# A four-layer network on one core: the last half batch leaves in two parts of 256 positions

## The chip, the cores and the metric

The kernel runs on one core of one Trainium2 chip. The core has five engines with a queue of instructions each: TensorE (PE, matrix products), VectorE (DVE), ScalarE (ACT), GpSimd (POOL) and SyncE (SP, which here issues the transfers). They wait for one another through semaphores. The metric is the time of one execution on the device in microseconds (us), lower is better. A trace of one profiled execution gives the start and the duration of each instruction; its span runs from the first to the last instruction.

## The reference, cut to what matters

The input is x of 8 batches, 512 channels and 32 x 32 = 1024 positions, fp32. Four layers follow one another. Layer 0 is an attention over 64 channels with a batch norm over the whole input, layer 1 a full attention over the positions, layers 2 and 3 are:

```python
# layer 2: t, p, g = the three projections of x (128 channels each)
s = softmax(t.T @ p * SCALE)
att = s @ g                      # 128 channels x 1024 positions
x = x + (Z_w @ att) * inv + shift
# layer 3
a = sign(x + rsign_bias)
y = (sign(W) * scale) @ a        # 512 x 512
s = batchnorm(y) + x
t = s - pr_shift
out = where(t > 0, t, pr_slope * t) + pr_bias
```

The change lies in the last product of layer 2 (by Z_w) and all of layer 3, for half of the positions of the batch that is worked on last.

## The kernel before, in words

The 512 channels lie as 4 blocks of 128 on the partitions; a position is a column. The 1024 positions are worked on in two halves of 512 columns (`HF`)[...]. `fast` does one batch. The batches come in a fixed order. In all but the last, the end of a batch is mixed with the products of the next batch, so that TensorE always has work. In the last batch (the `else` branch of `fast`, L994 to L1012) there is nothing to mix in but the end itself.

That end is, for each half h:

- `values2` (L954): the sum over positions of g times the exponentials, in one PSUM bank; DVE multiplies it by the inverse of the sums into `att` (L967).
- `close2` (L671): for each of the 4 blocks of channels, a product by z into a bank (L675, fp32; each product is two instructions on TensorE), and on DVE the sum with x, in place in `xt` (L677).
- `leave` (L679), a generator that stops at its `yield`s: 4 Signs on ACT (L686) make `sg` (f16). Then for each pair j of 0 and 1: a buffer `both` with members y1 (block j) and y2 (block j+2), and for each member a product of four f16 matmuls (L698) into a bank of its own. On DVE y = product x scale + x (L719). Then the last layer's rectifier, in one of two ways:
  - by way of POOL: DVE makes `up` (L725, both operands in SBUF), ACT makes y (L728, Identity), POOL adds them (L735), SyncE issues the output (L736);
  - by way of ACT and DVE: ACT makes `up` (L741, Relu), then y (L742, Identity), DVE joins them (L749), SyncE issues the output (L753).

The first way is taken where `h == 0 or j == 0` (L723), so only pair j1 of the second half goes the second way. Its last member y2 is cut in two there (L738, L739), each of 256 positions.

In the last batch the first half's `leave` is called `before`, the second half's `after`. The code's order is: verdict count (`count_bad`, a check of the softmax sums, one DVE group and one tiny product L789, read by L791), first half's Signs and its products j0 y1, j0 y2 and j1 y1, then the last two matmuls of `values2` of the second half with a stop in between, `close2` of the second half, the rest of `before`, and `after`. Within an engine the instructions run in an order that a scheduler makes from the program, with waits on semaphores where data or a buffer is shared.

Buffers that matter: 8 PSUM banks (tag `bank`) used in turn; 8 large buffers of tag `e` (exponentials, then `sg` and `both`); 3 buffers of tag `half_a`, in which `up` lies. A `tc.If` on the verdict follows (L1606); its body isn't run with this input.

Of the kernel before, what the change touches and what calls it, by code (L numbers as in the profile page):

```python
# [8 lines left out]
F32 = mybir.dt.float32  # L9
F16 = mybir.dt.float16  # L10
I32 = mybir.dt.int32
AF = mybir.ActivationFunctionType
ALU = mybir.AluOpType
# [3 lines left out]
P = 128  # L17
B = 8
C = 512
N = 1024  # L20
CC = C // P
NT = N // P
HF = 512
NH = N // HF
# [61 lines left out]
def kernel(  # L86
# [17 lines left out]
    nc = tc.nc  # L104
    mm = nc.tensor.matmul
# [17 lines left out]
    def bank():  # L123
        return psum["bank"].tile([P, HF], F32, tag="bank", name="bank")
# [17 lines left out]
    def half(i):  # L142
        return bass.ts(i, HF)
# [6 lines left out]
    sbw = {}  # L150
# [74 lines left out]
    def col(name, i):  # L225
        return ct[:, COL[name] + i : COL[name] + i + 1]
# [23 lines left out]
    ps3 = const.tile([P, CC], F32, tag="ps3", name="ps3")  # L250
    pb3 = const.tile([P, CC], F32, tag="pb3", name="pb3")
    rb3 = const.tile([P, CC], F32, tag="rb3", name="rb3")
    sa3 = const.tile([P, CC], F32, tag="sa3", name="sa3")
    cb3 = const.tile([P, CC], F32, tag="cb3", name="cb3")
# [413 lines left out]
            yield  # L668
        made.extend((tt, pt, gt))

    def close2(xt, att, h):  # L671

        for oc in range(CC):
            ps = bank()
            mm(out=ps, lhsT=sbw["z"][:, bass.ts(oc, P)], rhs=att, start=True, stop=True)  # L675
            xs = xt[:, oc, half(h)]
            nc.vector.tensor_tensor(xs, ps, xs, ALU.add)  # L677

    def leave(env, xt, dst, halves=range(NH), signs=None, stop=False):  # L679


        small = env["small"]
        for h in halves:
            sg = env["e"].tile([P, CC, HF], F16, tag="e", name="sg")
            for cc in range(CC):
                nc.scalar.activation(  # L686
                    sg[:, cc, :], xt[:, cc, half(h)], AF.Sign, bias=rb3[:, cc : cc + 1]
                )
            if stop:
                yield  # L690
            for j in range(CC // 2):
                both = env["e"].tile([P, 2, HF], F32, tag="e", name="both")
                y1, y2 = both[:, 0, :], both[:, 1, :]

                def product(lt):
                    ps = bank()
                    for cc in range(CC):
                        mm(  # L698
                            out=ps,
                            lhsT=lt[:, cc, bass.ts(j, P)],  # L700
                            rhs=sg[:, cc, :],
                            start=cc == 0,
                            stop=cc == CC - 1,
                        )
                    return ps

                if signs is None:
                    ps = product(sw3)
                    nc.scalar.activation(y2, ps, AF.Identity, bias=round3, scale=1.0 / PACK)
                    nc.vector.tensor_scalar(y2, y2, ROUND, None, ALU.subtract)  # L710
                    nc.vector.scalar_tensor_tensor(y1, y2, -PACK, ps, ALU.mult, ALU.add)
                    sums = y1, y2
                else:
                    sums = [product(signs[0])]
                    yield
                    sums.append(product(signs[1]))

                for y, ps, oc in ((y1, sums[0], j), (y2, sums[1], j + 2)):
                    nc.vector.scalar_tensor_tensor(  # L719
                        y, ps, sa3[:, oc : oc + 1], xt[:, oc, half(h)], ALU.mult, ALU.add  # L720
                    )
                    up = small.tile([P, HF], F32, tag="half_a", name="up3")
                    if signs is not None and (h == 0 or j == 0):  # L723

                        nc.vector.tensor_scalar(  # L725
                            up, y, nc3[:, oc : oc + 1], ps3[:, oc : oc + 1], ALU.max, ALU.mult
                        )
                        nc.scalar.activation(  # L728
                            y,
                            y,  # L730
                            AF.Identity,
                            bias=qb3[:, oc : oc + 1],
                            scale=col("L3_conv_pr_slope", oc),
                        )
                        nc.gpsimd.tensor_tensor(y, y, up, ALU.add)  # L735
                        nc.sync.dma_start(out=dst[:, oc, half(h)], in_=y)  # L736
                        continue
                    final = signs is not None and y is y2  # L738
                    for q in (slice(0, HF // 2), slice(HF // 2, HF)) if final else [slice(0, HF)]:  # L739
                        yq, uq = y[:, q], up[:, q]  # L740
                        nc.scalar.activation(uq, yq, AF.Relu, bias=cb3[:, oc : oc + 1])  # L741
                        nc.scalar.activation(  # L742
                            yq,
                            yq,
                            AF.Identity,
                            bias=pb3[:, oc : oc + 1],
                            scale=col("L3_conv_pr_slope", oc),
                        )
                        nc.vector.scalar_tensor_tensor(  # L749
                            yq, uq, ps3[:, oc : oc + 1], yq, ALU.mult, ALU.add  # L750
                        )
                        to = slice(h * HF + q.start, h * HF + q.stop)
                        nc.sync.dma_start(out=dst[:, oc, to], in_=yq)  # L753
                yield

    def unpacked(env):

        t = env["big"].tile([P, 2 * CC, N], F16, tag="h", name="signs")
        lo, hi = (t[:, i].rearrange("p (cc c) -> p cc c", c=C // 2) for i in range(2))
        near = env["big"].tile([P, 6, HF], F32, tag="hs", name="near")  # L760
        near = near[:, 0:2, :].rearrange("p i (cc c) -> p (i cc) c", c=C // 2)
        nc.vector.tensor_scalar(near, sw3, 1.0 / PACK, ROUND, ALU.mult, ALU.add)
        nc.vector.tensor_scalar(hi, near, ROUND, None, ALU.subtract)
        nc.vector.scalar_tensor_tensor(lo, hi, -PACK, sw3, ALU.mult, ALU.add)
        return lo, hi
# [28 lines left out]
    def channels(ap):  # L794
        return ap.rearrange("(cc p) n -> p cc n", p=P)
# [89 lines left out]
    def fast(env, n, hb, ua):  # L885
# [3 lines left out]
        xt = resident.pop(b)  # L889
# [47 lines left out]
        signs = None  # L937
        if more:
            steps = make_u(env, hb, got)
        else:  # L940
            signs = unpacked(env)

        def fill(k=1):
            for _ in range(k):
                next(steps, None)
# [26 lines left out]
        dst = channels(out[b])  # L972
        fill()
        values2(0, range(0, 2))
        if more:
            r = inverse_sums(env, esum, B + n)
            values2(0, range(2, NTH))
            att = values2(0, range(NTH, NT))
            values2(1, range(0, NTH))
            close2(xt, att, 0)  # L980
            att = values2(1, range(NTH, NT))
            fill()
            for _ in leave(env, xt, dst, [0]):
                fill()
            close2(xt, att, 1)
            rest3.append(leave(env, xt, dst, [1], stop=True))
            next(rest3[0])
            fill(2)
            for _ in steps:
                pass  # L990
        else:


            r = inverse_rows(env, esum, B + n)  # L994
            att = values2(0, range(2, NT))
            values2(1, range(0, 2))
            close2(xt, att, 0)
            values2(1, range(2, 6))
            before, after = leave(env, xt, dst, [0], signs), leave(env, xt, dst, [1], signs)
            count = count_bad(env)  # L1000
            next(count)
            next(before)
            next(before)
            att = values2(1, range(6, NT))
            next(before)
            close2(xt, att, 1)
            for _ in before:
                pass
            next(after)
            next(count)  # L1010
            for _ in after:
                pass  # L1012

        return hb, got[0] if more else None

# [107 lines left out]
    rest = [j for j in range(NPAIR) if j != order[0] // 2]  # L1123
# [6 lines left out]
    env = {}  # L1130
# [105 lines left out]
    for b in range(B):  # L1236
        xt = load_x(b) if b else first
# [145 lines left out]
    ps = bank()  # L1383
# [5 lines left out]
    ps = bank()  # L1389
# [5 lines left out]
    bias, gamma, beta = (ct[:, c0 + 2 * i : c0 + 2 * i + 2] for i in range(3))  # L1395
# [83 lines left out]
    with ExitStack() as main:  # L1479
# [3 lines left out]
        small = main.enter_context(tc.tile_pool(name="small", bufs=3))  # L1483
# [122 lines left out]
    with tc.If(verdict[0] > 0):  # L1606
        with (
# [5 lines left out]
            env = {"big": big, "e": epool, "small": small}  # L1613
# [4 lines left out]
            for b in range(B):  # L1618
                xt = load_x(b)
# [43 lines left out]
```

## Time and profile before

| | |
|---|---|
| time, median of 3 runs | 1901.04 us (1899.94 to 1901.69) |
| the profiled execution's own time | 1901.0 us |
| its span, first to last instruction | 1899.1 us |
| TensorE busy | 1878.7 us (99%), 6178 instructions |
| DVE busy | 1097.8 us (58%), 1762 instructions |
| ACT busy | 510.3 us (27%), 811 instructions |
| POOL busy | 223.5 us (12%), 176 instructions |
| `att` of the last half done (L967) | 1879.70 us |
| last L677 done | 1884.18 us |
| last L719 done | 1890.43 us |
| last L749 done | 1893.62 us |

The busy times are sums over the whole span. The part that the change touches is the last 20 us of it, and there the shares are other ones: between 1884 and 1888 us TensorE is busy 3.89, DVE 3.61, ACT 2.59 and POOL 1.31 of 4 us; between 1888 and 1892 us TensorE 0.26, DVE 3.07, ACT 2.98 and POOL 2.74 of 4 us. A row of a timeline gives start, duration, engine, line, operation and output<-inputs with their shapes, and in brackets the idle time before it with what ended it. `x2` means two instructions merged in one row, from the start of the first to the end of the second. Lines are those of the kernel before.

### The profile page before, as it was taken

Reading aid. Unit: us, or ns where it says so; the run is one execution under the profiler, and the core shown is the slowest. Engines: PE = TensorE matmul, PEld = TensorE weight load, DVE = VectorE, ACT = ScalarE, POOL = GpSimd, SP = SyncE. Lnnn points to the kernel's source line nnn. Section 1 sums busy time; section 2 is a strip of 40 time slices with the busy share of each in tenths; the row PEclk is TensorE's granted clock in tenths of the full one; section 3 lists DMA queues with packets and bytes.
Section 4 is the critical chain, followed back from the end, with each engine's and each line's share of the span. In section 5 each row is a group of like instructions: output and inputs, shape, how many; then the busy total and the mean of one; then the engine's idle time right before and its main releaser. Section 6 shows DMA issues by size and latency. Waiting matters only on the chain.

```text
span 1899.1 us, 16360 instructions
## 1 busy us (share of the span) xinstructions
PE 1878.7 (99%) x6178; PEld 973.4 (51%) x6178; DVE 1097.8 (58%) x1762; ACT 510.3 (27%) x811; POOL 223.5 (12%) x176
## 2 busy tenths in 40 slices
PE   9999999999999999999999999999999999999997
PEld 3366455544745446444645446544645455544653
DVE  3256576457663677438663675457753775466547
ACT  2142222144212432035202421144202521234013
POOL 0000111200121001200121001200130012101121
PEclk9999999999999999999999999999999999999999
DMA  8420000002000110002000110002000200000001
GB/s 322 159 78 6 1 17 1 1 23 78 17 1 1 45 61 12 1 12 89 17 1 0 49 57 12 0 23 78 12 0 12 89 12 0 1 33 22 12 0 47
DMA packets 25203, 66.52 MB, mean 35 GB/s; under 512 B 3552, under 2 KB 4764, under 8 KB 24476
## 3 DMA queue, kind: packets, MB, share of 16 engines
q1 hardware_dynamic: 24188, 64.96, 9.6%
q8 instruction: 51, 0.84, 0.2%
q10 hardware_dynamic: 864, 0.43, 0.1%
q14 instruction: 36, 0.29, 0.1%
q0 software_dynamic: 64, 0.00, 0.0%
HBM read 46.44 MB, written 18.94 MB: 34 GB/s over the span
## 4 chain that ended last, share of the span: by engine, by line
PE 92%; DVE 6%; issue 1%; ACT 1%; DMA 0%; POOL 0%; ACTq 0%; DVEq 0%
PE bank L388 42%; PE bank L557 20%; PE bank L958 6%; PE bank L806 6%; PE bank L1248 5%; PE bank L658 3%; PE bank L675 2%; PE bank L412 2%; PE wide L1288 1%; DVE both L749 1%; DVE both L719 1%; PE bank L1029 1%; PE wide L1342 1%; PE bank L1030 1%; PE bank L698 1%; DVE xt L677 1%
## 5 line engine op out<-in xcount | busy, mean ns | idle before, releaser
L557 PE MATMUL bank<-e,vt 128*128 128x512 f32 x768 | 334.2, 593 | 0.0
L557 PEld LDWEIGHTS bank<-e,vt 128*128 128x128 f32 x768 | 144.9, 190 | 174.8 <-issue 173.1
L388 PE MATMUL bank<-ut,h 128*128 128x512 f32 x384 | 182.3, 597 | 0.0
L345 DVE TENSOR_TENSOR e<-bank,e 128x512 f32<-128x512 f32 x128 | 87.9, 687 | 83.0 <-PE bank L388 82.8
L388 PE MATMUL bank<-us,hs 128*128 128x512 f32 x256 | 121.5, 597 | 1.4 <-DVE us L317 0.5
L388 PEld LDWEIGHTS bank<-ut,h 128*128 128x128 f32 x384 | 71.5, 190 | 95.6 <-issue 83.9
L958 PE MATMUL bank<-e,tpg 128*128 128x512 f32 x256 | 114.7, 595 | 0.0
L806 PE MATMUL bank<-tpg 128*128 128x512 f32 x256 | 114.6, 592 | 0.0
L813 ACT ACTIVATE e<-bank 128x512 f32<-128x512 f32 x128 | 76.4, 597 | 128.6 <-PE bank L806 128.6
L388 PE MATMUL bank<-wo,h 128*128 128x256 f32 x384 | 91.9, 382 | 0.0
L388 PE MATMUL bank<-h,wu 128*128 128x512 f32 x192 | 90.4, 593 | 0.7 <-ACT ut L350 0.7
L360 POOL TENSOR_TENSOR e<-e 128x512 f32<-128x512 f32 x32 | 43.3, 1354 | 403.9 <-ACT e L339 238.3
L818 DVE TENSOR_TENSOR esum<-esum,e 128x1024 f32<-128x1024 f32 x48 | 58.8, 1225 | 54.8 <-ACT e L813 54.8
L345 DVE TENSOR_TENSOR vt<-bank,vt 128x512 f32<-128x512 f32 x64 | 44.1, 689 | 69.8 <-PE bank L388 69.4
L806 PEld LDWEIGHTS bank<-tpg 128*128 128x128 f32 x256 | 48.6, 190 | 60.7 <-issue 60.5
L958 PEld LDWEIGHTS bank<-e,tpg 128*128 128x128 f32 x256 | 48.1, 190 | 60.4 <-issue 60.3
L360 POOL TENSOR_TENSOR ut<-ut 128x512 f32<-128x512 f32 x16 | 21.8, 1360 | 473.4 <-ACT ut L341 473.4
L388 PEld LDWEIGHTS bank<-wo,h 128*128 128x128 f32 x384 | 71.6, 190 | 11.4 <-issue 2.5
L388 PEld LDWEIGHTS bank<-us,hs 128*128 128x128 f32 x256 | 47.1, 190 | 54.9 <-issue 47.8
L686 ACT ACTIVATE sg<-xt,rb 128x512 f16<-128x512 f32 x64 | 45.0, 718 | 100.7 <-DVE xt L677 97.1
L1248 PE MATMUL bank<-xt,fg 128*64 128x512 f32 x256 | 59.1, 608 | 4.2 <-DMA fg<-in_w_fg 4.2
L658 PEld LDWEIGHTS bank<-tpg,xt 128*128 128x128 f32 x512 | 59.5, 192 | 7.2 <-issue 7.2
(333 smaller groups left out, 2965.6 us busy)
## 6 DMA issues: line engine op xcount, KB each, us to landing
xt<-in_x SPq DMA_DIRECT2D x55, 512.0 KB
out<-both SPq DMA_DIRECT2D x63, 256.0 KB
rfull<-r_dram SPq DMA_DIRECT2D x15, 512.0 KB
f_dram<-f SPq DMA_DIRECT2D x8, 256.0 KB
fb<-f_dram SPq DMA_DIRECT2D x8, 256.0 KB
w<-in_w SPq DMA_DIRECT2D x1, 1024.0 KB
q<-in_w_q SPq DMA_DIRECT2D x1, 1024.0 KB
k<-in_w_k SPq DMA_DIRECT2D x1, 1024.0 KB
```

The costliest lines, as they stand in the source:

```text
L345: nc.vector.tensor_tensor(dst, ps, u, ALU.add)
L360: nc.gpsimd.tensor_tensor(c22, c22, c12, ALU.add)
L388: mm(out=ps[:, q * w : (q + 1) * w], lhsT=lt(ka, kb, q, k), rhs=rhs(ka, kb, q, k), start=first and q == 0 and k == 0, stop=last and k == 1 ...
L412: mm(out=ps, lhsT=pv[side(h), bass.ts(oc, P)], rhs=f[side(h), :], start=True, stop=True,)
L557: mm(out=ps, lhsT=a[:, t, bass.ts(r_, P)], rhs=e[t], start=first and t == 0, stop=last and t == NTH - 1, skip_group_check=True,)
L658: mm(out=ps[:, i, :], lhsT=xt[:, cc, bass.ts(4 * h + i, P)], rhs=sbw["tpg"][:, cc, 2 * P : 3 * P], start=cc == 0, stop=cc == CC - 1,)
L686: nc.scalar.activation(sg[:, cc, :], xt[:, cc, half(h)], AF.Sign, bias=rb3[:, cc : cc + 1])
L806: mm(out=ps, lhsT=pt[:, 0, bass.ts(t, P)], rhs=tt[:, 0, half(h)], start=True, stop=True,)
L813: nc.scalar.activation(e[:, half(h)], ps, AF.Exp, scale=float(P) ** -0.5)
L818: nc.vector.tensor_tensor(esum, esum, e, ALU.add)
L958: mm(out=banks[h], lhsT=gt[:, t, :], rhs=es[t][:, half(h)], start=t == 0, stop=t == NT - 1,)
L1248: mm(out=banks[i][side(h), :], lhsT=w0[i][:, cc, :], rhs=xt[:, cc, half(h)], start=cc == 0, stop=cc == CC - 1,)
```

## The change

In the last batch, the second half goes through `close2` and `leave` in two parts of 256 positions (`quarters`). `close2` and `leave` take the columns as `ns`; everywhere else they get the full half, and the loop over halves stays as it was.

- The 4 products by z of 512 columns (L675) and their 4 sums (L677) become 8 of 256. The first part's come first; its Signs are put down in the code before the second part's products.
- Each part has its own `sg`, its own `both` buffers (the full size is taken from the pool, 256 columns are used), its own 4 Signs, 4 products (16 matmuls of 256 columns) and 4 L719 of 256.
- The condition for the way by POOL becomes `here.stop < N or j == 0`: the first part goes that way whole (4 members), the second part with pair j0 (2 members). Pair j1 of the second part goes by ACT and DVE, y1 and y2 each as one piece of 256; the cut of y2 falls away.
- The outputs are of 256 columns (128 KB): 8 for the half, where there were 3 of 256 KB and 2 of 128 KB.
- In the code's order both parts' products by z and Signs stand ahead of the rest of `before`.

```diff
-    def close2(xt, att, h):
+    def close2(xt, att, h, ns=slice(0, HF)):
         for oc in range(CC):
-            ps = bank()
-            mm(out=ps, lhsT=sbw["z"][:, bass.ts(oc, P)], rhs=att, start=True, stop=True)
-            xs = xt[:, oc, half(h)]
+            ps = bank()[:, ns]
+            mm(out=ps, lhsT=sbw["z"][:, bass.ts(oc, P)], rhs=att[:, ns], start=True, stop=True)
+            xs = xt[:, oc, h * HF + ns.start : h * HF + ns.stop]
             nc.vector.tensor_tensor(xs, ps, xs, ALU.add)
 
-    def leave(env, xt, dst, halves=range(NH), signs=None, stop=False):
+    def leave(env, xt, dst, halves=range(NH), signs=None, stop=False, ns=slice(0, HF)):
         small = env["small"]
         for h in halves:
-            sg = env["e"].tile([P, CC, HF], F16, tag="e", name="sg")
+            here = slice(h * HF + ns.start, h * HF + ns.stop)
+            sg = env["e"].tile([P, CC, HF], F16, tag="e", name="sg")[:, :, ns]
...
-                both = env["e"].tile([P, 2, HF], F32, tag="e", name="both")
+                both = env["e"].tile([P, 2, HF], F32, tag="e", name="both")[:, :, ns]
...
-                    ps = bank()
+                    ps = bank()[:, ns]
...
-                    up = small.tile([P, HF], F32, tag="half_a", name="up3")
-                    if signs is not None and (h == 0 or j == 0):
+                    up = small.tile([P, HF], F32, tag="half_a", name="up3")[:, ns]
+                    if signs is not None and (here.stop < N or j == 0):
...
-                    final = signs is not None and y is y2
-                    for q in (slice(0, HF // 2), slice(HF // 2, HF)) if final else [slice(0, HF)]:
-                        yq, uq = y[:, q], up[:, q]
-                        nc.scalar.activation(uq, yq, AF.Relu, bias=cb3[:, oc : oc + 1])
...
-                        nc.sync.dma_start(out=dst[:, oc, to], in_=yq)
+                    nc.scalar.activation(up, y, AF.Relu, bias=cb3[:, oc : oc + 1])
...
+                    nc.sync.dma_start(out=dst[:, oc, here], in_=y)
                 yield
...
-            before, after = leave(env, xt, dst, [0], signs), leave(env, xt, dst, [1], signs)
+            before = leave(env, xt, dst, [0], signs)
+            quarters = [slice(i * HF // 2, (i + 1) * HF // 2) for i in range(2)]
+            after = [leave(env, xt, dst, [1], signs, True, ns) for ns in quarters]
...
-            close2(xt, att, 1)
+            for ns, rest in zip(quarters, after):
+                close2(xt, att, 1, ns)
+                next(rest)
             for _ in before:
                 pass
-            next(after)
+            next(after[0])
             next(count)
-            for _ in after:
-                pass
+            for rest in after:
+                for _ in rest:
+                    pass
```

More of the change, by code (lines that the diff above doesn't have):

```diff
@@ L669, in project2 @@
         made.extend((tt, pt, gt))
-    def close2(xt, att, h):
+    def close2(xt, att, h, ns=slice(0, HF)):
         for oc in range(CC):
-            ps = bank()
-            mm(out=ps, lhsT=sbw["z"][:, bass.ts(oc, P)], rhs=att, start=True, stop=True)
-            xs = xt[:, oc, half(h)]
+            ps = bank()[:, ns]
+            mm(out=ps, lhsT=sbw["z"][:, bass.ts(oc, P)], rhs=att[:, ns], start=True, stop=True)
+            xs = xt[:, oc, h * HF + ns.start : h * HF + ns.stop]
             nc.vector.tensor_tensor(xs, ps, xs, ALU.add)
-    def leave(env, xt, dst, halves=range(NH), signs=None, stop=False):
+    def leave(env, xt, dst, halves=range(NH), signs=None, stop=False, ns=slice(0, HF)):
         small = env["small"]
         for h in halves:
-            sg = env["e"].tile([P, CC, HF], F16, tag="e", name="sg")
+            here = slice(h * HF + ns.start, h * HF + ns.stop)
+            sg = env["e"].tile([P, CC, HF], F16, tag="e", name="sg")[:, :, ns]
             for cc in range(CC):
                 nc.scalar.activation(
-                    sg[:, cc, :], xt[:, cc, half(h)], AF.Sign, bias=rb3[:, cc : cc + 1]
+                    sg[:, cc, :], xt[:, cc, here], AF.Sign, bias=rb3[:, cc : cc + 1]
                 )
@@ L719, in leave @@
                     nc.vector.scalar_tensor_tensor(
-                        y, ps, sa3[:, oc : oc + 1], xt[:, oc, half(h)], ALU.mult, ALU.add
+                        y, ps, sa3[:, oc : oc + 1], xt[:, oc, here], ALU.mult, ALU.add
                     )
-                    up = small.tile([P, HF], F32, tag="half_a", name="up3")
-                    if signs is not None and (h == 0 or j == 0):
+                    up = small.tile([P, HF], F32, tag="half_a", name="up3")[:, ns]
+                    if signs is not None and (here.stop < N or j == 0):
                         nc.vector.tensor_scalar(
@@ L735, in leave @@
                         nc.gpsimd.tensor_tensor(y, y, up, ALU.add)
-                        nc.sync.dma_start(out=dst[:, oc, half(h)], in_=y)
+                        nc.sync.dma_start(out=dst[:, oc, here], in_=y)
                         continue
-                    final = signs is not None and y is y2
-                    for q in (slice(0, HF // 2), slice(HF // 2, HF)) if final else [slice(0, HF)]:
-                        yq, uq = y[:, q], up[:, q]
[L741 to L752, printed above, removed]
-                        nc.sync.dma_start(out=dst[:, oc, to], in_=yq)
+                    nc.scalar.activation(up, y, AF.Relu, bias=cb3[:, oc : oc + 1])
+                    nc.scalar.activation(
+                        y,
+                        y,
+                        AF.Identity,
+                        bias=pb3[:, oc : oc + 1],
+                        scale=col("L3_conv_pr_slope", oc),
+                    )
+                    nc.vector.scalar_tensor_tensor(
+                        y, up, ps3[:, oc : oc + 1], y, ALU.mult, ALU.add
+                    )
+                    nc.sync.dma_start(out=dst[:, oc, here], in_=y)
                 yield
```

## The prediction

> **What bounds the kernel now.** I read the page first, then the chain of work that ended last, then the timelines of VectorE (DVE) and GpSimd (POOL) over the end, then the groups by shape. On the page TensorE is 99% busy, and the chain lies on it until 1884.33 us of a span of 1899.1. The change touches only what comes after att of the second half (L967, ends at 1879.70), and there the chain leaves TensorE:
>
> ```profile
> 1883.45 0.88 PE bank L698 x4
> ...
> 1887.13 0.72 DVE both L719 x2
> 1887.85 0.51 issue
> 1888.36 1.41 DVE up L725
> 1889.76 0.67 DVE both L719
> ...
> 1891.32 0.80 ACT up L741 x2
> 1892.12 0.50 ACT both L742
> ...
> 1893.13 0.48 DVE both L749
> ```
>
> From 1884.33 on the chain is on DVE, then ACT, then DVE. DVE has hardly a gap (timeline: start, duration):
>
> ```profile
> 1885.74 0.73 DVE L719 SCALAR_TENSOR_TENSOR both<-bank,sa,xt 128x512 f32<-128x512 f32 x1
> 1886.58 0.55 DVE L725 TENSOR_SCALAR up<-both,nc,ps 128x512 f32<-128x512 f32 x1
> 1887.04 1.41 DVE L719 SCALAR_TENSOR_TENSOR both<-bank,sa,xt 128x512 f32<-128x512 f32 x2
> 1888.36 1.41 DVE L725 TENSOR_SCALAR up<-both,nc,ps 128x512 f32<-128x512 f32 x1
> 1889.68 0.74 DVE L719 SCALAR_TENSOR_TENSOR both<-bank,sa,xt 128x512 f32<-128x512 f32 x1
> ```
>
> The same L725 takes 0.55 or 1.41. POOL's timeline says why:
>
> ```profile
> 1886.69 2.79 POOL L735 TENSOR_TENSOR both<-both,up 128x512 f32<-128x512 f32 x2 [2.71 <-ACT both L728]
> 1890.69 1.27 POOL L735 TENSOR_TENSOR both<-both,up 128x512 f32<-128x512 f32 x1 [1.21 <-ACT both L728]
> ```
>
> The two additions end at 1889.48, the L725 that began at 1888.36 ends 0.29 later. L719 (one input in PSUM) ran at 0.70 each under the same POOL work.
>
> After the last L749 (ends 1893.62) SyncE issues the last output. The DMA queue's own waits:
>
> ```profile
> SPq L1606 <- SPq L1606: 2.9, 1, 2.9
> ```
>
> SyncE waits 2.9 us for the last transfer (columns: total, times, longest); in all 5.5 us lie between the last L749 and the end of the span. Groups by shape (busy us, mean ns of one) give the prices:
>
> ```profile
> L719 DVE SCALAR_TENSOR_TENSOR both<-bank,sa,xt 128x512 f32<-128x512 f32 x8 | 5.9, 744 | 0.7 <-PE bank L698 0.7
> ...
> L742 ACT ACTIVATE both<-both,pb,ct 128x256 f32<-128x256 f32 x2 | 1.1, 585 | 0.0
> ...
> L749 DVE SCALAR_TENSOR_TENSOR both<-up,ps,both 128x256 f32<-128x256 f32 x2 | 1.0, 484 | 0.1
> ...
> L741 ACT ACTIVATE up<-both,cb 128x256 f32<-128x256 f32 x2 | 0.9, 492 | 0.0
> ```
>
> [...]
>
> **The change part by part.** Below, h0 is the first half, q0 and q1 the two parts, j0/j1 the pairs, y1/y2 the members. Starts of successive DVE instructions stand 0.60 (L677), 0.66 (L719) and 0.46 us (L725) apart at 512; the pair 0.744/0.484 gives 1.04 ns a column, so 0.33 and 0.39 at 256. L725 gets 0.52 ns a column (L463 in this trace: 805 ns at 1024 columns, 543 at 512), so 0.33, and 0.41 in full.
>
> 1. *Products by z.* 4 of 512 become 8 of 256. A pair of fp32 matmuls costs 0.86 at 512; 256-column fp32 matmuls elsewhere (L388) follow at 0.216 each, so 0.43: no loss on TensorE. The first result is there at 1880.45 instead of 1880.87. But L677 can't yet run at its own 0.33: it follows TensorE's 0.43. The eighth product needs the PSUM bank of h0's j1 y1 product, which DVE in the new order reads only after six L677. So it waits until 1883.74 and holds back h0's j1 y2 product behind it on TensorE: that L719 starts at 1885.39 instead of 1884.35.
> 2. *DVE occupancy.* L677 4 x 0.60 to 8 x 0.33: +0.27. L719 4 x 0.66 to 8 x 0.39: +0.51. L725 2 x 0.46 to 6 x 0.33: +1.04, since all of q0 and j0 of q1 now end through DVE, ACT and POOL. Sum +1.82.
> 3. *POOL.* After att, 4 additions of 512 (5.0 us) become 2 of 512 and 6 of 256 (6.9). Each L725 of the y2 kind falls behind a y1 addition that has just begun. Laying the four engines' instructions out in their new order with these prices (the same for the kernel before ends at 1893.62, as traced), L725 of h0 j1 y2 comes at 1886.50 while POOL runs 1886.35 to 1887.61; q0 j0 y2 at 1888.92 in 1888.83 to 1890.09; q0 j1 y2 at 1891.27 and q1 j0 y2 at 1893.01 meet the short ones. Stalls 0.84, 0.91, 0.30, 0.30 = 2.35, against 0.43 + 0.86 = 1.29 before: +1.06. The ring of three up buffers adds a wait: ACT's Relu of q1 j1 y1, its sum ready at 1893.1, waits for the addition of q0 j1 y2 (ends 1893.57), and ACT's last three operations queue behind it. That costs 0.24 and is in the sums.
> 4. *Idle DVE at the start and at the eighth product*, less gaps that the new interleaving fills: +0.80.
> 5. *The tail after the last L719.* Before: 1890.43 to 1893.62, 3.19. After, from the last L719 (ends 1894.11): ACT still owes a Relu and two Identity at 256, then L749: end 1896.48, 2.37. -0.82.
> 6. *Signs, f16 products, SyncE.* Signs 4 become 8 of 0.50 on an ACT that waits for L677. Products: 16 matmuls at 0.215 become 32; whether at 0.11 or 0.20 each, TensorE runs ahead of DVE. Outputs: 9 issues become 12, of 0.33 to 0.62 us, at least 0.7 apart; SyncE's read of the verdict now stands before h0's third output, but its L790 is done by 1886.2, the output ready at 1887.6. All hidden by DVE; if it weren't, each issue would cost 0.4.
> 7. *The last transfers.* Before, 768 KB were issued within 1.8 us and moved at some 350 GB/s until 1895.25. After, 128 KB come every 0.8 us, so the last one waits for none: -0.3 (0 to -0.6).
>
> Sum: 1.82 + 1.06 + 0.80 - 0.82 - 0.3 = +2.56 us. The profiled execution took 1901.0 (span 1899.1 and 1.9 around it), the runs' median is 1901.04; both give 1903.6.
>
> Bounds: POOL at 0.63 (half of 1.26) gives +2.1; at 1.26 (no gain from width) +5.2.
>
> **The rivals.** *POOL dear*: an addition of 256 costs over 1.0 us[...]. Then POOL's six additions pace the end: at 0.9 the layout gives +3.2, at 1.26 +5.2, so from 1.0 on it is more than 0.2% slower. For it: no 256-column addition in the trace, and 128x4 powers that take 1.0. [...] Time 1906.
>
> *Milder lock*: the additions miss the L725s, since a shift of 0.2 us decides which starts first. With no stalls at all the layout ends at 1895.18: +1.3 with the transfers, 1902.3. Against: y2 follows y1 by about the time ACT takes.
>
> *The earlier start wins*: the first Sign starts at 1880.96 instead of 1882.47 and the tail is 0.82 shorter; if DVE had slack, the end came about 1.1 earlier, 1899.9. Against: between 1879.70 and 1890.43 DVE is busy 10.07 of 10.73 us (busy time by stretch), and point 2 alone takes the gain back. That the change doesn't do what it says is no rival: the built order of the new kernel has the narrow forms on every engine, and nothing ahead of att moves.
>
> **How the numbers follow.** This kernel's measurement can tell 0.2% (3.8 us) from no change. Forecast 0.60: 1903.6, its own range 1902.3 to 1904.8, and 0.05 of it above. POOL dear 0.18. Milder lock 0.15. Earlier start 0.07, of which 0.02 more than 3.8 us faster (over a quarter of the 13.9 us that the stage lasts). Slower: 0.18 + 0.05 = 0.23; faster 0.02; the same 0.75. The range 1901.2 to 1905.8 leaves out most of the earlier start and the upper half of POOL dear.
>
> **What would show it.** Last L749 at 1896.5; six POOL additions of 256 at 0.73; four L725 of y2 stretched beyond 0.41 (0.55), each ending with or after a POOL addition; six L677 about 0.43 apart, then a gap before the eighth; the wait after the last output under 2.9. Wrong it would be if DVE before the last L719 ended by 1891.5, or if POOL ran gapless to the end.

## The result and the profile after

The changed kernel takes 1903.57 us (median of 21 runs, 1902.38 to 1904.23) against 1901.04 (21 runs, 1899.94 to 1901.92) for the kernel before: a ratio of 1.0013, 95% interval 1.0007 to 1.0019. It is slower by 2.5 us, surely, and within 0.2%. The profiled execution took 1903.26 us, its span is 1901.5.

For all comparisons below, M is the time in the profiled execution from the end of the last half's `att` to the end of the last DVE instruction that makes an output of it: the stage until the last sum y = product x scale + x ends, plus the tail after it. Nothing ahead of `att` is changed, so M sees the change without what the whole program scatters. It is worked out from rows rounded to 0.01, so that its last digit is good to 0.01 or so.

| us | before | after |
|---|---|---|
| end of `att` | 1879.70 | 1879.61 |
| stage, to the end of the last L719 (after: L720) | 10.72 | 14.11 |
| tail, to the end of the last L749 (after: L747) | 3.20 | 2.41 |
| M | 13.92 | 16.52 |
| from there to the end of the span | 5.48 | 5.37 |
| DVE busy in the stage | 10.07 | 13.28 |
| POOL busy in the stage | 5.71 | 7.97 |

Lines of the changed kernel: L720 is the sum (before L719), L726 `up` on DVE (L725), L729 ACT's Identity on the way by POOL (L728), L736 POOL's addition (L735), L739 and L740 ACT's Relu and Identity (L741, L742), L747 the join (L749). The chain of work that ended last (start, duration, engine, output, line) now runs like this after `att`:

```profile
1880.40 0.42 DVE xt L677
...
1880.83 0.42 DVE xt L677
...
1882.98 0.66 DVE both L720
1883.64 0.66 DVE xt L677 x2
1884.31 0.45 DVE up L726
1884.76 0.66 DVE both L720
...
1888.35 1.31 DVE up L726
...
1890.36 0.73 POOL both L736
...
1891.41 0.81 DVE up L726
1892.22 0.80 DVE both L720 x2
...
1894.01 0.59 ACT both L740
1894.59 0.41 ACT up L739
...
1895.02 0.61 ACT both L740
...
1895.65 0.48 DVE both L747
```

As before, DVE sets the pace up to the last sum; then come operations of ACT and DVE's last join. An addition of POOL has entered the chain, but it did not hold up the L726 behind it, which began 0.39 after the L720 before it (1890.70), as the sums here follow one another too. On DVE's timeline there is no gap from 1882.90 until the last sum ends at 1893.72, so every stretched instruction in this stretch counts in full. The `up`s are the place to look:

```profile
1885.79 1.52 DVE L726 TENSOR_SCALAR up<-both,nc,ps 128x512 f32<-128x512 f32 x1
...
1887.23 0.40 DVE L726 TENSOR_SCALAR up<-both,nc,ps 128x256 f32<-128x256 f32 x1
...
1888.35 1.30 DVE L726 TENSOR_SCALAR up<-both,nc,ps 128x256 f32<-128x256 f32 x1
...
1889.57 0.81 DVE L726 TENSOR_SCALAR up<-both,nc,ps 128x256 f32<-128x256 f32 x1
...
1891.09 0.40 DVE L726 TENSOR_SCALAR up<-both,nc,ps 128x256 f32<-128x256 f32 x1
...
1891.41 0.81 DVE L726 TENSOR_SCALAR up<-both,nc,ps 128x256 f32<-128x256 f32 x1
```

They belong, in this order, to h0 j1 y2, q0 j0 y1, q0 j0 y2, q0 j1 y1, q0 j1 y2 and q1 j0 y1; the seventh (q1 j0 y2, at 1892.93) took 0.40. The same instruction takes 0.40 or two to three times as long. POOL's timeline of the same time:

```profile
1885.77 1.26 POOL L736 TENSOR_TENSOR both<-both,up 128x512 f32<-128x512 f32 x1 [4.50 <-ACT both L729]
1888.24 1.26 POOL L736 TENSOR_TENSOR both<-both,up 128x512 f32<-128x512 f32 x1 [1.21 <-ACT both L729]
1889.46 0.77 POOL L736 TENSOR_TENSOR both<-both,up 128x256 f32<-128x256 f32 x1
1890.36 0.73 POOL L736 TENSOR_TENSOR both<-both,up 128x256 f32<-128x256 f32 x1
1891.18 0.89 POOL L736 TENSOR_TENSOR both<-both,up 128x256 f32<-128x256 f32 x1
...
1893.01 0.90 POOL L736 TENSOR_TENSOR both<-both,up 128x256 f32<-128x256 f32 x1
```

Each long L726 began while an addition ran and ended 0.15 to 0.28 us after it: 1885.79 in the addition of 1885.77, 1888.35 in that of 1888.24, 1889.57 in that of 1889.46, 1891.41 in that of 1891.18. The L726 of 1891.09 began before POOL and kept its 0.40; there the addition took 0.89 instead of 0.73, and the one of 1893.01, behind the L726 of 1892.93, took 0.90. Over the prediction's prices, 0.55 (512 columns) and 0.41 (256), the four long L726 stand at +0.97, +0.89, +0.40 and +0.40 = 2.66.

SyncE's wait after the last output is what it was in the kernel before:

```profile
SPq L1608 <- SPq L1608: 2.9, 1, 2.9
```

This wait is no sharp measure: in the traces of all the kernels below it is 2.5 to 2.9 us, in whichever way the outputs are cut.

### The profile page after: what moved, and what is told of

Same layout as the page of the kernel before. It is cut to its first block, busy times and chain, and to the rows that moved or that the text cites. A ratio compares the mean times of both kernels' runs of the same rounds, so it can differ in the third digit from the quotient of the medians.

```text
span 1901.5 us, 16446 instructions
## 1 busy us (share of the span) xinstructions
PE 1878.2 (99%) x6202; PEld 979.2 (51%) x6202; DVE 1099.7 (58%) x1773; ACT 511.9 (27%) x817; POOL 225.4 (12%) x180
## 4 chain that ended last, share of the span: by engine, by line
PE 92%; DVE 6%; issue 1%; ACT 1%; DMA 0%; POOL 0%; DVEq 0%; ACTq 0%
PE bank L388 42%; PE bank L557 20%; PE bank L955 6%; PE bank L803 6%; PE bank L1250 5%; PE bank L658 3%; PE bank L412 2%; PE bank L675 1%; PE wide L1290 1%; DVE both L747 1%; DVE both L720 1%; PE bank L1031 1%; PE wide L1344 1%; PE bank L1032 1%; DVE xt L677 1%; PE bank L699 1%
## 5 line engine op out<-in xcount | busy, mean ns | idle before, releaser
L687 ACT ACTIVATE sg<-xt,rb 128x512 f16<-128x512 f32 (+1 forms) x68 | 46.0, 693 | 102.3 <-DVE xt L677 98.7
```

What stands on the lines that cost most here:

```text
L687: nc.scalar.activation(sg[:, cc, :], xt[:, cc, here], AF.Sign, bias=rb3[:, cc : cc + 1])
```

## The experiments

Each kernel differs from the one before or the one after in what its diff shows. In the last column is the ratio of its time to the kernel before with its 95% interval (the kernel before, run beside them, had medians of 1900.98 to 1901.21).

| run | stage + tail | M | ratio of times |
|---|---|---|---|
| before | 10.72 + 3.20 | 13.92 | |
| after | 14.11 + 2.41 | 16.52 | 1.0013 [1.0007, 1.0019] |
| e1 second ring for `up` | 14.12 + 2.36 | 16.48 | 1.0012 [1.0005, 1.0018] |
| e2 order alone | 10.78 + 3.51 | 14.29 | 1.0002 [0.9993, 1.0010] |
| e3 after, `up` on ACT | 8.89 + 7.29 | 16.18 | 1.0007 [0.9999, 1.0016] |
| e4 after, POOL only in the first half | 13.37 + 3.16 | 16.53 | 1.0015 [1.0009, 1.0022] |
| e5 products by z and Signs alone in two parts | 10.61 + 3.78 | 14.39 | 1.0003 [0.9995, 1.0011] |
| e6 only from the Signs on in two parts | 13.42 + 2.42 | 15.84 | 1.0010 [1.0003, 1.0016] |
| e7 before, `up` on ACT | 9.27 + 4.64 | 13.91 | 0.9999 [0.9991, 1.0008] |
| e8 before, one `up` on ACT | 9.41 + 3.98 | 13.39 | 0.9995 [0.9986, 1.0003] |
| e9 after without POOL's additions | 11.39 + 2.41 | 13.80 | 1.0001 [0.9992, 1.0009] |
| e10 before without POOL's additions | 9.72 + 3.42 | 13.14 | 1.0000 [0.9992, 1.0009] |
| e11 e8, pair j1 without Relu on ACT | 9.41 + 3.58 | 12.99 | 0.9997 [0.9989, 1.0006] |
| e12 the same for j1 y2 alone | 9.41 + 3.54 | 12.95 | 0.9996 [0.9988, 1.0005] |

Of the experiments the times separate e1, e4 and e6 from the kernel before, and no others. The verdicts below therefore rest on M and on the rows of the traces, one profiled execution each. How well the stage repeats can be seen where kernels have the same instructions on DVE up to the last sum: 9.41 in e8, e11 and e12, 14.11 and 14.12 in the changed kernel and in e1. The end behind M repeats less well, 5.0 to 5.9 us over all fourteen traces, and is not part of M.

**The ring of `up` buffers (e1).** The changed kernel, with three further buffers for the second part:

```diff
-                    up = small.tile([P, HF], F32, tag="half_a", name="up3")[:, ns]
+                    up = small.tile([P, HF], F32, tag="half_b" if ns.start else "half_a", name="up3")[:, ns]
```

> The second part's up buffers come from the other ring of three (tag half_b), so no up waits for an addition three before it; DVE's order stays as in the changed kernel. Measure M: from the end of the last att to the end of the last join (before 13.92 us, changed 16.52). The prediction's step 3 put 0.24 on the ring: M 16.3 and about 1903.3 us. My theory now ([...]the ring idle in the trace): M 16.5 +- 0.15, time as the changed kernel, 1903.5.

M is 0.04 shorter. The Relu that was said to wait for a buffer did not: in the changed kernel the addition that held the buffer (1892.20) ended at 1892.93, before the Relu's own sum (1892.54, 0.47 long) was ready at 1893.01, and the Relu began at 1893.10; with the second ring it began at 1893.01, with the sum ready at 1892.98. In the changed kernel the ring cost nothing worth naming.

**The new order alone (e2).** The changed code with one part of 512, and the last member cut in two as before:

```diff
-            quarters = [slice(i * HF // 2, (i + 1) * HF // 2) for i in range(2)]
+            quarters = [slice(0, HF)]
```

> The changed kernel's code order (second half's products by z and Signs ahead of the rest of the first half), but one part of 512 instead of two of 256, the last member cut as before. Theory 'narrow forms cost': M as before, 13.9 +- 0.5, time 1901.0. Rival 'the order costs' (the first half's rest is held back): M at least 15.5, time 1902.5 or more.

+0.37 in M, and no difference in time that could be told: with whole tiles the order alone costs a small part of the 2.60. Here the ring does show: ACT's Relu of 1890.59 stood idle for 0.68 until an addition had released an `up` buffer. The stalls are other ones too (two L726 of 1.01 and 0.78), so M of this version is not a term that could be taken out of the 2.60.

**One half of the parts at a time (e5, e6).** e5 is the kernel before, with `close2` and the Signs in two parts (two runs of four Signs) and all after them whole; e6 is the changed kernel with `close2` whole. First e5's edit (that of the Signs is left out), against the kernel before, then e6's, against the changed one:

```diff
-            close2(xt, att, 1)
+            for i in range(2):
+                close2(xt, att, 1, slice(i * HF // 2, (i + 1) * HF // 2))
```

```diff
-            for ns, rest in zip(quarters, after):
-                close2(xt, att, 1, ns)
+            close2(xt, att, 1)
+            for rest in after:
                 next(rest)
```

> The kernel before, with only the products by z, their sums and the Signs of the last half in two parts of 256; products, up, joins and outputs whole, code order as before. Theory 'narrow forms cost': eight sums instead of four (+0.27) and DVE tied to TensorE's pace, no gain from the earlier first Sign: M 14.2 (13.9 to 14.8), time 1901.3. Rival 'the earlier start gains': M 13.4 or less.

> The changed kernel with the products by z and the sums of the last half whole (512), two parts from the Signs on. Theory: occupancy of the narrow L720 and L726 (+0.51 +1.04)[...] are here, less 0.8 of tail: M 15.8 (15.2 to 16.4), so most of the loss. Rival 'the loss is at the start' (sums at TensorE's pace, idle DVE): M 14.6 or less.

e5 costs 0.47 and e6 1.92 over the kernel before. Both numbers came as the theory expected, but e5's not in the way it said: its stage is 0.11 shorter, and its tail is 0.58 longer. The order on DVE and the stalls changed with the edit (the two L725 that had lost 0.43 and 0.86 are now two of 0.82 and 1.23, 0.97 over their own time), so 0.47 is what this version costs and not the price of narrow sums. An earlier first product bought nothing that can be seen in M. e6 alone has most of the loss, from the Signs on.

**Without POOL's additions (e9, e10).** The same line is taken out of both kernels, so the outputs that go by POOL lack the term `up`; all the rest of the work is there.

```diff
-                        nc.gpsimd.tensor_tensor(y, y, up, ALU.add)
```

> The changed kernel without POOL's additions of the last batch (the outputs that go by POOL lack the up term): DVE and ACT keep every instruction in the same order[...]. This prices the stalls alone. Theory 'stalls are part, narrow forms the larger part': M falls by the stalls' 1.3 from 16.5 to 15.2 (14.8 to 15.6), still 1.9 over the next kernel. Rival 'stalls are nearly all of the loss': M about that of the next kernel, within 0.5.

> The kernel before without POOL's additions of the last batch (the same term left out). Its L725 can't stall: M from 13.9 to 13.2 (12.9 to 13.4). If ACT sets the end anyway, as putting every up on ACT suggested, M 13.8 or more.

DVE and ACT keep the order of their instructions in both. e10 came as expected. e9 came neither as the theory had it (15.2) nor within the 0.5 of e10 that the rival allowed: M is 13.80, 0.66 over e10 and so much nearer to the rival. DVE's timeline of e9:

```profile
1885.48 0.53 DVE L726 TENSOR_SCALAR up<-both,nc,ps 128x512 f32<-128x512 f32 x1
...
1887.04 0.39 DVE L726 TENSOR_SCALAR up<-both,nc,ps 128x256 f32<-128x256 f32 x1
1887.36 0.40 DVE L726 TENSOR_SCALAR up<-both,nc,ps 128x256 f32<-128x256 f32 x1
...
1890.22 0.47 DVE L720 SCALAR_TENSOR_TENSOR both<-bank,sa,xt 128x256 f32<-128x256 f32 x1
```

No L726 is longer than its own 0.40 (0.53 at 512), and the last sum ends at 1890.69. The instruction that took 1.41 in the kernel before takes 0.54 in e10:

```profile
1888.38 0.54 DVE L725 TENSOR_SCALAR up<-both,nc,ps 128x512 f32<-128x512 f32 x1
```

So the additions cost the changed kernel 16.52 - 13.80 = 2.72 in M. All of it lies in the stage (the tail is 2.41 in both), and the four long L726 make it up, row against row: 1.52 - 0.53, 1.30 - 0.39 and twice 0.81 - 0.40. The additions cost the kernel before 13.92 - 13.14 = 0.78: 1.00 in the stage, of which its tail, set by ACT, gives back 0.22. Of the loss of 2.60, 1.94 is dearer stalls behind POOL, and 13.80 - 13.14 = 0.66 is all the rest: narrow forms, order, the shorter tail. This carries the main finding, and here the times agree: e9 has a median of 1901.20 us (1900.14 to 1901.79), below every run of the changed kernel (1902.38 to 1904.23), with the kernel before at 1901.05 beside the one and 1901.04 beside the other.

**`up` on ACT (e3, e7).** DVE then has no instruction on the way by POOL but the sum. Relu takes `up` with scale and a bias of its own, as y times slope:

```diff
-                        nc.vector.tensor_scalar(
-                            up, y, nc3[:, oc : oc + 1], ps3[:, oc : oc + 1], ALU.max, ALU.mult
-                        )
+                        nc.scalar.activation(
+                            up, y, AF.Relu, bias=ub3[:, oc : oc + 1], scale=ps3[:, oc : oc + 1]
+                        )
...
-                            bias=qb3[:, oc : oc + 1],
+                            bias=pb3[:, oc : oc + 1],
```

with `ub3` = `qb3` - `pb3` made once at the start; e3 is this edit in the changed kernel, e7 in the one before.

> The changed kernel with up made by ACT (Relu with scale and bias) instead of DVE for every member that goes by POOL[...]. Theory[...]: DVE loses some 6 x 0.33 + 2 x 0.46 of work and 2.7 of stalls, ACT gains 8 x 0.4 to 0.6 and becomes the bound: M 15.3 (14.7 to 15.8), time about 1902.2. Rival 'ACT and POOL chains pace it anyway': M 16.5 or more.

> The kernel before with up made by ACT for every member of the last batch that goes by POOL. If [...]DVE set the end before as well: M 13.4 (13.0 to 13.8), ACT the new bound, time about 1900.5. If they don't: ACT's 0.6 per member is added to its chain, M 14.5 or more.

Both missed. ACT's timeline of e3 says why:

```profile
1889.95 1.08 ACT L730 ACTIVATE both<-both,pb,ct 128x256 f32<-128x256 f32 x2
1890.94 1.08 ACT L727 ACTIVATE up<-both,ub,ps 128x256 f32<-128x256 f32 x2
1891.92 1.08 ACT L730 ACTIVATE both<-both,pb,ct 128x256 f32<-128x256 f32 x2
1892.90 0.94 ACT L740 ACTIVATE up<-both,cb 128x256 f32<-128x256 f32 x2
1893.75 1.08 ACT L741 ACTIVATE both<-both,pb,ct 128x256 f32<-128x256 f32 x2
```

Each row starts before the one above it has ended, and so it goes from 1885.45 on, but for one gap of 0.03. ACT had become the bound, the last sum on DVE (8.89 after `att`) was 5.2 us earlier than in the changed kernel, and the tail of 7.29 was ACT's. In e7 too the stage gained 1.45 and the tail gave it back. The theory had left out ACT's own length, so these two runs say nothing on the stalls; e9 was made for that reason.

**Only the first half by POOL (e4).** The second half then goes by ACT and DVE in both parts:

```diff
-                    if signs is not None and (here.stop < N or j == 0):
+                    if signs is not None and h == 0:
```

> The changed kernel with both parts wholly by ACT and DVE (no addition on POOL after the first half's). DVE has the same number of narrow instructions, six joins at 0.39 instead of six up at 0.33. Theory[...]: the stalls that parts' additions cause (0.40 + 0.40 + 0.08, and knock-ons) go, the two with the first half's additions stay: M 15.7 (15.2 to 16.1). Rival 'occupancy alone': six times 0.06 more, M 16.9.

A miss as well, for theory (15.7) and rival (16.9) alike: 16.53. DVE's timeline, POOL's and ACT's, in this order:

```profile
1886.53 1.52 DVE L726 TENSOR_SCALAR up<-both,nc,ps 128x512 f32<-128x512 f32 x1
...
1889.43 1.10 DVE L747 SCALAR_TENSOR_TENSOR both<-up,ps,both 128x256 f32<-128x256 f32 x1 [0.20 <-ACT both L740]
```

```profile
1888.98 1.26 POOL L736 TENSOR_TENSOR both<-both,up 128x512 f32<-128x512 f32 x1 [1.21 <-ACT both L729]
```

```profile
1890.28 0.51 ACT L739 ACTIVATE up<-both,cb 128x256 f32<-128x256 f32 x1 [0.48 <-POOL both L736]
...
1892.20 0.60 ACT L740 ACTIVATE both<-both,pb,ct 128x256 f32<-128x256 f32 x1
1892.71 0.89 ACT L739 ACTIVATE up<-both,cb 128x256 f32<-128x256 f32 x2
1893.51 1.08 ACT L740 ACTIVATE both<-both,pb,ct 128x256 f32<-128x256 f32 x2
1894.49 0.89 ACT L739 ACTIVATE up<-both,cb 128x256 f32<-128x256 f32 x2
1895.29 1.08 ACT L740 ACTIVATE both<-both,pb,ct 128x256 f32<-128x256 f32 x2
```

The additions of the first half alone still stretched an L726 by 0.97 (1.52 instead of 0.55) and a join by 0.62 (1.10 instead of 0.48). ACT, with 16 narrow operations, stood idle for 0.48 until the second of these additions had released an `up` buffer, so that here the ring did cost time, and from there on it had no pause longer than 0.03.

**Versions of the kernel before (e8, e11, e12).** e8 takes the edit of e7 for a single member, y2 of pair j0 of the second half (`on_act = h == 1 and y is y2`, within the way by POOL). e11 also gives pair j1 its `up` by DVE's instruction and a plain addition on DVE as the join (its Identity then takes the bias `qb3`); e12 does so for j1 y2 alone. The edit of both against e8, without the condition that picks the members:

```diff
-                        nc.scalar.activation(uq, yq, AF.Relu, bias=cb3[:, oc : oc + 1])
+                        nc.vector.tensor_scalar(
+                            uq, yq, nc3[:, oc : oc + 1], ps3[:, oc : oc + 1], ALU.max, ALU.mult
+                        )
...
-                        nc.vector.scalar_tensor_tensor(
-                            yq, uq, ps3[:, oc : oc + 1], yq, ALU.mult, ALU.add
-                        )
+                        nc.vector.tensor_tensor(yq, yq, uq, ALU.add)
```

> The kernel before with one up alone on ACT, that of j0 y2 in the last half, whose L725 stalled 0.86 behind POOL. Theory: DVE loses 0.46 + 0.86 ahead of the last L719, ACT gains one Relu in a gap: M 13.3 (13.1 to 13.6), time 1900.4. If the stall was free (ACT sets the end): M 13.9 or more.

> The kernel before with one up (j0 y2 of the last half) on ACT as in the run with M 13.39, and both members of j1 with up on DVE and a plain sum as join, so ACT loses three Relus from a tail in which it never paused (1887.6 to 1892.96). Theory 'ACT sets that tail': M 12.9 (12.6 to 13.2), time about 1899.7. If DVE's ups stall behind POOL's last two additions: M 13.4 or more.

> As the last one, but only j1 y2 (two parts of 256) has its up on DVE; y1 keeps its Relu on ACT. M 13.1 (12.8 to 13.4): ACT loses two Relus of 0.40, DVE gains two up of 0.33, one of which may wait for POOL.

In e8 the `up` that was stretched to 1.41 is on ACT, and DVE goes on with the last sum in the meantime; ACT's row, then DVE's:

```profile
1888.35 0.80 ACT L728 ACTIVATE up<-both,ub,ps 128x512 f32<-128x512 f32 x1
```

```profile
1888.75 0.74 DVE L720 SCALAR_TENSOR_TENSOR both<-bank,sa,xt 128x512 f32<-128x512 f32 x1
...
1891.20 1.15 DVE L756 SCALAR_TENSOR_TENSOR both<-up,ps,both 128x512 f32<-128x512 f32 x1 [1.71 <-ACT both L749]
```

The last sum began 9.98 us after `att` in the kernel before and begins at 8.66 now, earlier by the 1.32 that the expectation names (0.46 + 0.86); ACT's tail takes 0.78 of it back, and M is 0.53 shorter. All three came within 0.15 of the M expected, e11 in part by luck: the stalls that were to bring 13.4 or more came too, in two of its three `up`s (0.75 at 512 columns, and the following one of 256):

```profile
1890.06 1.41 DVE L751 TENSOR_SCALAR up<-both,nc,ps 128x256 f32<-128x256 f32 x1
```

e12 is shorter by 0.97 in M, its median 1900.05 against 1901.05, and its interval still includes no difference: these versions are promising by their rows, and not shown faster.

## Why the prediction was right

1903.6 was predicted, 1903.57 measured; the class (slower by less than 0.2%) and the kind of mechanism (DVE bound, narrow forms and stalls behind POOL against a shorter tail) hold. The weights do not: narrow forms and idle DVE were put too high, the stalls too low. Of its signs, six additions of 0.72 to 0.73 of POOL's own time and four stretched `up`s came (two of these at y1, not at y2); the gap before the eighth L677 and a last wait under 2.9 did not. The terms, measured by the two kernels and by e9 and e10:

| term, us | predicted | measured | from |
|---|---|---|---|
| 2, DVE occupancy | +1.82 | +1.63 | DVE busy in the stage, e9 10.56, e10 8.93 |
| 4, idle DVE | +0.80 | +0.04 | idle in the stage, e9 0.83, e10 0.79 |
| 3, stalls | +1.06 | +1.72 | stage: (14.11 - 11.39) - (10.72 - 9.72) |
| 5, tail | -0.82 | -0.79 | 2.41 - 3.20 |
| 7, last transfers | -0.3 | -0.11 | 5.37 - 5.48 |
| sum | +2.56 | +2.49 | |

The sum is nearly exact because errors cancel: -0.95 in terms 2 and 4, +0.66 in term 3, +0.22 in the other two. That it came so close is luck.

- **Point 1.** The six L677 came 0.43 apart (1880.40 to 1882.56), as said. The wait of the eighth product for a bank did not occur: its second instruction on TensorE began at 1883.01, while DVE was still reading the bank of h0's j1 y1 (L720, 1882.90 to 1883.64), so it lay in another one:

```profile
1883.01 0.38 PE L675 MATMUL bank<-att,z 128*128 128x256 f32 x1
```

```profile
1882.90 0.74 DVE L720 SCALAR_TENSOR_TENSOR both<-bank,sa,xt 128x512 f32<-128x512 f32 x1
```

The product of h0's j1 y2 followed on TensorE from 1883.22, and its L720 began at 1884.67, not at 1885.39. The step that failed is the count of the banks in turn; in what turn they were taken instead is not shown.
- **Point 4.** It was built on that wait. In the changed kernel 0.79 of the 0.83 us of idle DVE lie between `att` and the first L677, and the kernel before had nearly as much in all (0.65), only in other places.
- **Point 2** was right in size, less 0.19. Its spacings came out (L677 0.33, L720 0.39, `up` 0.32 apart at 256 columns), although 0.744/0.484 gives 1.02 ns a column and not 1.04, and sets a sum with one input in PSUM beside a join with both in SBUF; the sum itself takes 0.74 and 0.47 in the changed kernel. DVE's busy time counts the six L677 at TensorE's pace (0.42 each), so terms 2 and 4 are told apart only roughly. Together they are 1.67 instead of 2.62.
- **Point 3, POOL's price.** 0.73 for an addition of 256 columns was the author's estimate, a shape that no trace of the kernel before shows; measured it is 0.72 to 0.73 where DVE did not interfere (0.77 to 0.90 where it did). The rival *POOL dear* falls with it.
- **Point 3, the stalls.** The first two came in their places and sizes (0.84 and 0.91 predicted, 0.97 and 0.89 measured). Of the next ones the layout said q0 j1 y2 and q1 j0 y2, 0.30 each; it was q0 j1 y1 and q1 j0 y1, 0.40 each. At 1889.46 POOL went on from one addition to the next without a pause, and DVE's L726 came 0.11 later. The rows sum to 2.66 (2.35 predicted). Nearly half of the error (0.29 of 0.66) is on the other side: the 1.29 of the kernel before were counted in full, but without POOL's additions its stage is only 1.00 shorter (e10). The L725 at 1880.65, stretched to 0.98, has cover, as its rows have it: of the four L677 behind it the last, at 1883.49, is back on TensorE's pace (it begins 0.05 after the one before has ended), and the L719 behind them starts 4.65 us after `att` with the stretch as without it (e10).
- **Point 3, the ring.** Its 0.24 was not there (e1); in the orders of e2 and e4 a wait of that kind did occur (0.68 and 0.48).
- **Point 5** was right to 0.03, by its own instructions: a Relu and two Identity on ACT, then the join.
- **Point 6** held: no row of it stands in the chain. Of **point 7** nothing can be told: the end was 0.11 shorter and the wait for the last transfer stayed at 2.9, where less was said, but over the kernels of this case the end scatters by more than the 0.3 that was predicted (5.0 to 5.9 us).
- **The rivals.** *Milder lock* put the end without stalls 1.6 us later than before; e9 shows it 0.1 earlier in M (13.80 against 13.92). It did not occur, but had it occurred, the change would have cost about nothing by M. The forecast missed this in two ways that cancel. Its layout ends 15.48 after `att` without stalls, 1.68 later than e9, and 16.78 with them: 2.35 of stalls cost it only 1.30, where the measured ones cost their full 2.72. What was to cover the rest of them in the layout is not on record. *The earlier start wins* falls with e5 (14.39, where 13.4 or less was said) and with e9 beside e10: without any stall the changed kernel is still 0.66 longer.

In every one of the six meetings above the one that came second, by 0.02 to 0.23 us, was stretched: the four L726 by 0.40 to 0.97, the two additions by 0.16 and 0.17. POOL was first in four of them. What the two engines share is not shown.

## What to carry to other kernels

DVE and POOL take turns on the same data here, and with the tiles cut in two the stretched `up`s of the stage went from two (0.98 and 1.41) to four; a short DVE instruction lasted until a longer addition had ended (1.30 instead of 0.40, for an L726 that began 0.11 after an addition of 1.26). Count such meetings from a layout of both engines, and take the additions out once to see what they cost in all (0.78 before, 2.72 after). The stalls in the kernel before came to 1.29 by their rows, but without the additions its stage was only 1.00 shorter (e10): what is covered has no price, so a difference of two sums of stalls must not be taken from rows alone. And before work is moved off a bound engine, add up the engine that receives it: twice here ACT took back most or all of what DVE gained (4.88 of 5.22 us in e3, 1.44 of 1.45 in e7).

## What the runs showed of the hardware

- An addition of two SBUF operands on POOL, fp32, took 1.26 us at 512 columns and 0.72 at 256: 2.1 ns a column and some 0.18 fixed, by these two numbers.
- The loss at a meeting is uneven. A DVE instruction that came second lost up to 0.97 us (1.52 instead of 0.55), while an addition that came second lost 0.16 (0.89 instead of 0.73), behind an L726 of 0.40 that had begun 0.09 before.
- An ACT operation with bias from a column took 0.49 us at 256 columns (L741 of the kernel before), one with bias and scale from columns 0.58 (L742). At 512 columns a Relu with bias from a column took 0.72 (L741 of the kernel before), one with bias and scale from columns 0.80 (L728 of e8). Whole, the pair of one member (Relu and Identity) took 0.72 and 0.80 in the kernel before; cut in two, twice 0.49 and twice 0.58, which is part of what filled ACT in e3 and e4.
- No dependence of the program's end on the cut of the last outputs can be seen. From the last DVE instruction it took 5.48 us with 768 KB issued shortly before and 5.37 with 128 KB every 0.8 us, and over all fourteen traces 5.0 to 5.9 with the first cut and 5.0 to 5.8 with the second.
